# Five bias loads of set-up: begun behind the landing of x of batch 0, in place of first on GpSimd's queue

## The chip, the cores and the metric

The kernel runs on one core of one Trainium2 chip. The metric is the device time of one execution in microseconds (us), median of three. A profiled execution gives a trace; its engines are PE (TensorE matmuls), PEld (TensorE weight loads), DVE (VectorE), ACT (ScalarE), POOL (GpSimd) and SP (SyncE). A letter q behind an engine's name means its queue of instructions, which also issues DMAs. "L199" is line 199 of the kernel before the change.

## What is computed

Two graph layers on x of shape 32 x 512 x 512 in float32, with one adjacency matrix adj of 512 x 512 for all 32 batches:

```python
h = jnp.maximum(_layernorm(x, axis=-1), 0.0)
x = x + _L0_gnn_ref(h, adj, L0_gnn_weight, L0_gnn_bias)
h = jnp.maximum(_layernorm(x, axis=-1), 0.0)
x = x + _L1_gnn_ref(h, adj, Wq, bq, Wk, bk, Wv, bv, Wo, bo)
```

Layer 0 is `(adj @ h) @ weight + bias`. Layer 1 is attention with 8 heads, whose scores get `(1 - adj) * -1e9` added, so that with these weights of adj each row's softmax picks the one key with the largest entry of adj. The attention then is a choice of rows, and its two products with Wv and Wo fold into one with Wv @ Wo. The biases bq and bk enter only through a bound that says whether this short cut holds.

## The kernel before

Set-up (lines 73 to 310) runs once. It loads the weights, adj and x of the first batches into SBUF, multiplies Wv by Wo into `wvo` on TensorE, transposes adj into `adjT`, finds each row's largest entry of adj, checks that the short cut holds (`flag`), and computes batch 0's normalization and its product with adj. Then a value that all engines load from `flag` picks a path, and `single_path` runs over the 32 batches, with a list of work per batch written out step by step. TensorE is fed there by products of 128x128 by 128x256 and the like.

The whole of set-up is under a manual schedule: each engine runs its instructions in the order in which the program writes them, and waits on semaphores for what it reads. So the place of a line in the program is its place in its engine's queue.

The loads of set-up, by queue:

- SyncE: half of Wv's rows 0 to 255 (line 90); Wo's first and third 128 rows and Wv's third (line 93); adj and x of batch 0 in two halves each (line 96, `adj_s` and `xs[0]`); wq, wk, the weight of layer 0 `w0_s`, and x of batch 1 (line 98), 1 MB each.
- ScalarE: the other half of Wv's rows 0 to 255, Wo's second and fourth 128 rows, Wv's fourth (lines 90 and 93).
- GpSimd: after the identity matrix and two constants (lines 99 to 101) the five bias loads of lines 198 to 201: `bv_c`, `bt[0]` (bq) and `bt[1]` (bk) as columns, 512 values each spread over 128 partitions, so that neighbours in a partition lie 128 values apart in memory; `b0_r` and `cvo` (bo) as one row of 2 KB repeated to 128 partitions, 256 KB each in SBUF. They are written far down in the program, but nothing of GpSimd stands before them except the constants, and they wait for nothing.

TensorE's queue starts with twenty transposes of the identity (line 170), then `turn(0, 0)` and `turn(0, 1)`, which transpose Wv's rows 0 to 255 (line 126), one product (`fold`, line 150), `turn(1, 0)` and `turn(1, 1)` with Wv's rows 256 to 511, and the other products of Wv @ Wo with seven block products in place of eight. ScalarE and VectorE copy the transposes to `wvT` (lines 130 and 131), VectorE forms sums of blocks (line 141, and lines 329 to 335 in `sum_a`), and adds products up (lines 184, 205, 214). Then come the largest entries of adj (`peaks`, lines 157 and 158), the statistics of x (lines 361 to 370), the transposes of adj (line 115) and the product with adj (line 271).

Readers of the biases: `bt` is read by ScalarE at line 241, `bv_c` by VectorE at lines 162 and 164, `cvo` at line 293, and `b0_r` at line 300. `w0_s` is first read by sums at lines 341 and 343, x of batch 1 at line 394. Line 673 is the first product of batch 0 in `single_path`, line 312 the load of `flag` on every engine.

Of the kernel before, what the change touches and what calls it, by code (L numbers as in the profile page):

```python
# [8 lines left out]
F32 = mybir.dt.float32  # L9
# [9 lines left out]
P = 128  # L19
# [7 lines left out]
def gnn_two_layers(ctx: ExitStack, tc: tile.TileContext, x, adj, w0, b0, wq, bq, wk, bk, wv, bv, wo, bo, out):  # L27
# [15 lines left out]
    nc = tc.nc  # L43
    B, N, D = x.shape
    C = N // P
# [4 lines left out]
    def big(name):  # L50
        return keep.tile([P, C, N], F32, name=name)

    xs, hs = [big(f"x{i}") for i in range(5)], [big(f"h0_{i}") for i in range(2)]
# [19 lines left out]
    with ExitStack() as tmp, tc.manual_schedule():  # L73
        look = tmp.enter_context(tc.tile_pool(name="look", bufs=1))
# [4 lines left out]
        wt = [look.tile([P, DC, D], F32, name=f"wt{i}") for i in range(2)]  # L79
        bt = [look.tile([P, DC], F32, name=f"bt{i}") for i in range(2)]  # L80
        bv_c = look.tile([P, DC], F32, name="bv_c")
        wvT = yT
        wvT_t = xs[2].rearrange("p c (a n) -> p c a n", a=2)
        wo_t = wvo_t.rearrange("p t c (k n) -> p t c k n", k=2)
# [110 lines left out]
        norms[0].offset()  # L195
        norms[1].stats(1)
        norms[1].power()
        for t, d in ((bv_c, bv), (bt[0], bq), (bt[1], bk)):
            nc.gpsimd.dma_start(t, d.rearrange("(c p) -> p c", p=P))  # L199
        for d, r in ((b0, b0_r), (bo, cvo)):  # L200
# [1462 lines left out]
```

## Time and profile before

| | |
|---|---|
| median of three executions | 1021.16 us (1020.17 to 1023.55) |
| the profiled execution's own time | 1016.16 us |
| its span, first to last instruction | 1014.4 us |
| mean granted TensorE clock | 0.992 |
| GpSimd issues its first bias load at | 1.61 us |
| GpSimd issues its fifth bias load at | 4.62 us |
| bv from issue to landing | 6.4 us |
| b0 from issue to landing | 8.1 us |
| first product of batch 0 (line 673) | 45.27 us |

Times within an execution count from the start of the span. The busy shares of a page are averages over the whole span; set-up is its first 45 us, so what happens in it has to be read from the timeline and from tables of short windows. In a table of windows each engine has its busy time and, in brackets, its instructions; then follow the granted TensorE clock (1.00 is full), the mean busy share of the 16 DMA engines, and GB/s. In a view of the DMA queues, q1 holds SyncE's transfers, q10 ScalarE's, and q0 GpSimd's; the last figure is the time that their packets took, as a share of 16 engines over the window. Packets that overlap on an engine can bring the sum over 100%.

### The profile page before, as it was taken

The numbers are of one execution on the slowest core, as the hardware profiler recorded it, in microseconds if no ns is written. First come the engines' busy times: TensorE is split into PE (matmuls) and PEld (weight loads), VectorE is DVE, ScalarE is ACT, GpSimd is POOL, SyncE is SP. The second block draws the span as 40 slices with busy tenths as digits, with TensorE's granted clock in tenths as the row PEclk, the third lists the DMA queues.
The fourth block names the chain that finished last, engine by engine and source line by source line (L and its number), as shares of the span: only waits on it lengthen the run. The fifth ranks groups of instructions, "written<-read, shape, count | busy, mean of one in ns | idle before, by whom it ended". The sixth has DMA issues, their size and how long they took to land.

```text
span 1014.4 us, 17265 instructions
## 1 busy us (share of the span) xinstructions
PE 988.0 (97%) x5627; PEld 886.9 (87%) x5627; DVE 801.9 (79%) x1792; ACT 586.1 (58%) x1282; POOL 591.1 (58%) x666
## 2 busy tenths in 40 slices
PE   7999999998999999999999999999999999999994
PEld 6468999897999999999999999999999999999882
DVE  4998897667888877778887777788877777888773
ACT  2765364556755555667655555676555556675330
POOL 1032366656666666666666666666766666667543
PEclk8999999999999999999999999999999999999998
DMA  9214558788888888888888888998888888888867
GB/s 312 82 65 152 113 164 250 220 223 219 207 226 206 201 221 209 231 221 207 211 194 207 219 207 227 225 223 202 201 203 213 209 219 227 221 209 207 210 209 265
DMA packets 161884, 208.90 MB, mean 206 GB/s; under 512 B 16556, under 2 KB 104376, under 8 KB 161784
## 3 DMA queue, kind: packets, MB, share of 16 engines
q0 software_dynamic: 44544, 120.10, 48.5%
q1 hardware_dynamic: 115480, 85.66, 29.2%
q10 hardware_dynamic: 1760, 1.93, 0.5%
q8 instruction: 46, 0.75, 0.3%
q14 instruction: 54, 0.44, 0.2%
HBM read 123.55 MB, written 84.09 MB: 205 GB/s over the span
## 4 chain that ended last, share of the span: by engine, by line
PE 72%; DMA 2%; POOL 2%; issue 2%; DVE 1%; ACT 1%; SPq 0%; POOLq 0%; ACTq 0%; DVEq 0%
PE mm L532 50%; PE mm L652 13%; PE mm L655 7%; PE mm L649 2%; DMA hc<-hs 1%; POOL x L495 1%; DMA pi<-posd,idx 1%; DMA z<-zr 1%; DMA hs<-h,dest 0%; POOL hs L692 0%; POOL out_dram L516 0%; POOL yT L495 0%; PE mm L727 0%; ACT h L379 0%; DVE st L361 0%
## 5 line engine op out<-in xcount | busy, mean ns | idle before, releaser
L588 DVE TENSOR_TENSOR x<-mm,x 128x512 f32<-128x512 f32 x217 | 148.8, 686 | 130.2 <-PE mm L532 128.2
L495 POOL DMA_INDIRECT x<-z,pplace x96 | 153.5, 1599 | 81.8 <-ACT yT L660 40.9
L379 ACT ACTIVATE h<-x,off,rstd 128x512 f32<-128x512 f32 x256 | 196.1, 804 | 7.3 <-DVE off L370 4.0
L532 PE MATMUL mm<-w_t,sel 128*128 128x256 f32 x744 | 171.7, 380 | 1.3 <-DVE x L588 1.3
L365 ACT ACTIVATE rstd<-mv,eps 128x2 f32<-128x2 f32 (+1 forms) x90 | 26.3, 292 | 241.8 <-DVE mv L362 241.8
L532 PEld LDWEIGHTS mm<-w_t,sel 128*128 128x128 f32 x744 | 140.6, 190 | 21.4 <-DVE x L588 2.5
L361 DVE BATCH_NORM_STATS2 st<-x 128x6 f32<-128x512 f32 x234 | 157.7, 674 | 1.1
L652 PE MATMUL mm<-ap,h 128*128 128x256 f32 x648 | 157.8, 380 | 0.0
L516 POOL DMA_INDIRECT out_dram<-x,xi x100 | 124.8, 1248 | 42.5 <-DVE zs L578 21.0
L495 POOL DMA_INDIRECT x<-in_x_dram,xi x108 | 104.0, 963 | 72.5 <-DVE x L588 37.4
L652 PEld LDWEIGHTS mm<-ap,h 128*128 128x128 f32 x648 | 114.9, 191 | 11.1
L495 POOL DMA_INDIRECT at<-in_x_dram,gi x81 | 76.9, 949 | 72.8 <-DVE st L361 25.0
L532 PE MATMUL mm<-w_s,yT 128*128 128x256 f32 x496 | 117.3, 379 | 0.8 <-ACT zs L580 0.8
L532 PE MATMUL mm<-hTs,wvo_t 128*128 128x168 f32 x720 | 113.4, 307 | 2.4 <-ACT zs L580 1.4
L532 PEld LDWEIGHTS mm<-hTs,wvo_t 128*128 128x128 f32 x720 | 105.4, 190 | 3.1 <-ACT zs L580 1.9
L580 ACT ACTIVATE zs<-mm,cvo_c 128x168 f32<-128x168 f32 x240 | 83.0, 398 | 38.2 <-PE mm L532 37.8
L532 PEld LDWEIGHTS mm<-w_s,yT 128*128 128x128 f32 x496 | 92.8, 190 | 12.3 <-ACT zs L580 1.0
L655 PEld LDWEIGHTS mm<-ag,adjT 128*128 128x128 f32 x648 | 89.3, 191 | 5.6
L655 PE MATMUL mm<-ag,adjT 128*128 128x128 f32 x648 | 89.7, 275 | 0.0
L627 DVE TENSOR_TENSOR x<-x,b_r 128x512 f32<-128x512 f32 x124 | 84.0, 678 | 0.0
L660 ACT COPY yT<-mm 128x512 f32<-128x512 f32 x108 | 61.5, 571 | 29.6 <-PE mm L655 29.6
L532 PE MATMUL mm<-hT,wvo 128*128 128x168 f32 x480 | 78.3, 306 | 0.0
(323 smaller groups left out, 1678.7 us busy)
## 6 DMA issues: line engine op xcount, KB each, us to landing
hc<-hs SPq DMA_DIRECT2D x124, 176.0 KB
z<-zr SPq DMA_DIRECT2D x120, 96.0 KB
hs<-h SPq DMA_DIRECT2D x52, 192.0 KB
z<-zr SPq DMA_DIRECT2D x120, 80.0 KB
hs<-h SPq DMA_DIRECT2D x52, 160.0 KB
out_dram<-x SPq DMA_DIRECT2D x26, 256.0 KB
x<-in_x_dram SPq DMA_DIRECT2D x12, 256.0 KB
x<-xn SPq DMA_DIRECT2D x8, 256.0 KB
```

Source lines behind the costliest of these rows:

```text
L361: self.nc.vector.bn_stats(st, self.src[:, self.chunks[i], :])
L365: self.nc.scalar.activation(self.rstd[:, 0:len(self.chunks)], self.mv[:, :, 1], AF.Sqrt, bias=self.eps)
L379: self.nc.scalar.activation(dst, src, AF.Relu, bias=self.off[:, i:i + 1], scale=self.rstd[:, i:i + 1])
L495: return behind(nc.gpsimd.indirect_dma_start(out=dst, out_offset=None, in_=rows, in_offset=bass.IndirectOffsetOnAxis(ap=at, axis=0), **more))
L516: stored = behind(nc.gpsimd.indirect_dma_start(out=out_rows, out_offset=bass.IndirectOffsetOnAxis(ap=plan.xi[:, b, c:c + 1], axis=0), in_= ...
L532: nc.tensor.matmul(bank[:, m, 0:half], lhs[:, k, m * P:(m + 1) * P], rhs[:, k, :], start=(first and m == 0 and k == 0), stop=(k == 1), ski ...
L580: taken = nc.scalar.activation(dst[:, m, :], bank[:, m, :], AF.Identity, bias=cvo_c[:, 2 * i + m:2 * i + m + 1])
L588: return nc.vector.tensor_add(dst, bank, dst)
L627: nc.vector.tensor_add(X[b][:, c, :], X[b][:, c, :], b0_r)
L652: nc.tensor.matmul(two(bank, j), H0[b][:, j, cols], two(plan.ap[:, j, :], j), start=False, stop=False, skip_group_check=True)
L655: nc.tensor.matmul(bank[:, j * P:(j + 1) * P], extra[:, j - 1, cols], plan.ag[:, j - 1, j * P:(j + 1) * P], start=False, stop=(j == C - 1) ...
L660: tick(nc.scalar.copy(yT[:, d, :], bank))
```

## The change

A tile `hold` of one column is new. Before its five loads GpSimd copies one column of x of batch 0 into it, from the last 128 rows. These come with the second of x's two halves, so the copy waits for that DMA; the loads stand behind it in GpSimd's queue. Nothing reads `hold`. The order on the other engines and queues is as before. Behind the five loads, GpSimd's next instruction is the load of `flag` (line 312).

```diff
         bv_c = look.tile([P, DC], F32, name="bv_c")
+        hold = look.tile([P, 1], F32, name="hold")
...
         norms[1].power()
+        nc.gpsimd.tensor_copy(hold, xs[0][:, C - 1, 0:1])
         for t, d in ((bv_c, bv), (bt[0], bq), (bt[1], bk)):
             nc.gpsimd.dma_start(t, d.rearrange("(c p) -> p c", p=P))
         for d, r in ((b0, b0_r), (bo, cvo)):
```

## The prediction

> **What bounds the kernel now.** I read the page first, in the order of its parts: the busy shares, then the 40 slices.
>
> ```profile
> PE 988.0 (97%) x5627; PEld 886.9 (87%) x5627; DVE 801.9 (79%) x1792; ACT 586.1 (58%) x1282; POOL 591.1 (58%) x666
> ...
> PE   7999999998999999999999999999999999999994
> ...
> PEclk8999999999999999999999999999999999999998
> ```
>
> TensorE is busy at 9 tenths or more almost throughout; only the first slice (25.4 us) shows both a low share and a low clock. The change sits in that slice. So the question is what set-up waits for, and whether an earlier end of set-up is kept: after it TensorE is the bound, nothing there runs by an absolute clock, and a shift of its first batch matmul should reach the end in full.
>
> Next, the timeline of TensorE alone through set-up (start, duration, engine, line, what it writes and reads, count, and in brackets idle time and releaser):
>
> ```profile
> 5.08 1.04 PE L126 MATMUL pt<-ident,x 128*128 128x128 f32 x8
> 6.14 2.02 PE L150 MATMUL mm<-x,yT 128*128 128x256 f32 x8
> 11.70 0.47 PE L126 MATMUL pt<-ident,x 128*128 128x128 f32 x1 [3.53 <-DMA x<-in_L_gnn_Wv_dram]
> 12.38 1.75 PE L126 MATMUL pt<-ident,x 128*128 128x128 f32 x7 [0.21 <-DMA x<-in_L_gnn_Wv_dram]
> 13.93 3.62 PE L150 MATMUL mm<-x,yT 128*128 128x256 f32 x8
> 17.34 3.96 PE L150 MATMUL mm<-wvo_t,x 128*128 128x256 f32 x16
> ...
> 45.27 4.96 PE L673 MATMUL mm<-w_s,yT 128*128 128x512 f32 x11 [0.72 <-ACT yT L274]
> ```
>
> One long stall, 3.53 us, for rows 256 to 511 of Wv. From 11.70 on there is no other stall of that kind until 45.27, where batch 0 begins. The same shapes also run slower after the stall: 8 products in 3.62 us against 2.02 us before it. A table of the granted clock shows why (columns: busy time and count of PE, PEld, DVE, ACT, POOL, then the clock, DMA share, GB/s):
>
> ```profile
> 8.00:10.00 2.00, 0.17 (x1) 0.00 (x0) 1.07 (x2) 0.59 (x1) 0.00 (x0) 1.00 1.01 318
> 10.00:12.00 2.00, 0.30 (x1) 0.18 (x1) 0.82 (x2) 0.00 (x0) 0.00 (x0) 0.80 0.83 203
> 12.00:14.00 2.00, 1.79 (x9) 1.62 (x9) 0.00 (x0) 0.65 (x2) 0.00 (x0) 0.50 0.98 339
> ...
> 16.00:18.00 2.00, 2.00 (x6) 1.56 (x5) 1.28 (x3) 0.00 (x0) 0.00 (x0) 0.50 1.05 393
> ```
>
> The clock is halved soon after the stall and is full again by about 18.2. Last, what the DMA engines did while TensorE stalled, from 6 to 12 us:
>
> ```profile
> DMA packets 795, 1.51 MB, mean 251 GB/s; under 512 B 178, under 2 KB 178, under 8 KB 795
> ...
> q0 software_dynamic: 230, 0.48, 48.3%
> q1 hardware_dynamic: 300, 0.55, 27.5%
> q10 hardware_dynamic: 265, 0.48, 21.8%
> ```
>
> q0 is GpSimd's queue, so the bias loads: they hold 48.3% of the 16 engines for 6 us and move only 0.48 MB. q1 (SyncE) and q10 (ScalarE), which carry Wv and Wo, get the rest. The same view gives 367 GB/s from 4 to 6.4 us, before q0 sets in, and 376 GB/s from 12 to 28 us, after it.
>
> [...] Here 3.53 us of idleness is followed by 0.50. [...]
>
> **The change, part by part.**
> *Removed from the start.* By 6.4 us, 0.54 (2 to 4 us) and 0.88 MB have moved, 1.42 MB of the 2.10 MB of Wv and Wo (eight transfers of 256 KB, with 2 MB counted as 2.10). Without q0 the other 0.68 MB takes 0.68/0.367 = 1.85 us. q1 lacks 0.30 MB and q10 0.38 MB: at half the rate each, q1 has its last at about 8.0, and q10, sharing with adj at the end, at about 8.5. From last byte to transposes took up to 1 us (q10's last packets lie in the slice 10 to 12, its reader starts at 12.38) on disturbed engines; I take 0.6, so the two readers can start at 8.7 and 9.2 in place of 11.70 and 12.38. TensorE is free at 8.16, so this stands. Gain 3.2 us.
> *Clock.* With 0.5 us idle in place of 3.5 the clock should stay full. 7 transposes then take 7/8 of 1.04 = 0.9 us, not 1.75; 8 products 2.0, not 3.62. TensorE is then done with them at 9.2 + 0.9 + 2.0 = 12.1, and line 150's sixteen start there in place of 17.34: 5.2 us earlier.
> *What is late next.* VectorE. ScalarE's four copies follow the transposes at 0.27 us each and end at about 10.95 (14.82 before), so line 329 starts at 11.0 for 14.85; after three sums of 0.69 it meets line 184, whose 0.72 us wait for products is gone. From there it is 4.5 us ahead, line 362's last ends at 19.0 for 23.48, and line 205 begins at 19.1 for 24.01, without its 0.53 us wait: 4.9 us ahead. TensorE waits for VectorE at lines 265 and 270 (0.26 and 0.76 us before), so the smaller shift rules: **4.9 us**.
> *adj and x.* They follow on q1: 2.10 MB more at 376 GB/s is 5.6 us, so x's second half has landed at 8.25 + 5.6 + 0.6 = 14.4. Line 361 wants it at 17.0 (21.54 less 4.5), adj's first half is wanted at 14.3 and lands near 10.3. No new wait.
> *Added: the copy.* No GpSimd copy is in the trace. A memset of 128x1 took 0.10 us there; I bound the copy by 0.1 and 0.6 (the larger selects of the same engine took 0.58) and take 0.2. It blocks GpSimd from about 1.6 to 14.4; behind it are only the five loads, then the flag at 41.8, so nothing else is held.
> *Moved: the loads.* Their issues took 0.95, 0.80, 0.77, 0.58, 0.58, in sum 3.68 us: 14.6 to 18.3. Landing took 6.4 us for bv and 8.1 for b0. So bv lands at 21.0, bq 21.9, bk 22.7, b0 25.2, bo 25.7. The readers, 4.9 or 5.0 us earlier than before: bq at line 241 25.2, bv at line 162 26.5, bk 27.7, bo at line 293 35.2, b0 at line 300 38.3. The tightest slack is bq's 3.3 us.
> *What they now collide with.* wq, wk, w0 and x of batch 1, 4.2 MB, alone from 13.8 to 25.0. The bias traffic costs what it cost before: 0.53 MB is 1.4 us, and 5.6 us at 244 in place of 376 GB/s (6.4 to 12 us) is 2.0 us; so they end by about 28.4. x of batch 1 is read at line 394, 36.64 less 4.9 = 31.7, and w0 at 31.9. Hidden, with 3.3 us to spare. If that cover failed, each us of lateness beyond it would come off the gain.
>
> Against the profiled execution (1016.16 us, span 1014.4) the sum is 1016.16 - 4.9 = 1011.3. The median is 5.0 us above that execution, and I take the shift from the median: 1021.16 - 4.9 = **1016.3 us**.
>
> **The rivals.**
> *The clock falls all the same.* [...] For it: TensorE was busy only 3.6 of the 6.8 us before the drop. [...] If half clock still covers about 11.4 to 18.2, it then covers dense work: 6.8 us of it loses 3.4, so 5.2 - 3.4 = 1.8 us are left, 1019.4.
> *The weights aren't limited by q0.* Then Wv comes no sooner, the stall stays, and the time is 1021.2 as before. Against it: q1 and q10 together moved 1.03 MB in the 6 us, 172 GB/s, where they had 367 without q0. A half effect, 2.4 us, gives 1018.8.
> *The wait moves to the biases: slower.* Place: ScalarE's line 241 for bq. VectorE is busy while GpSimd issues, among it tensor_scalar and two-input operations, and SyncE has 4.2 MB queued. From 25.2 on each us of lateness costs a us; at 30.1 the gain is used up. bq would need 14.6 us from issue at 15.5, against 6.4 to 8.1 measured. Later in the kernel GpSimd's indirect transfers land in 3.3 to 7.5 us beside a busy VectorE and 80% DMA load, which speaks against it. Landing at 32 gives 1021.16 + 1.9 = 1023.1.
>
> **How the numbers follow.** About 0.3%, 3.1 us, is what a measurement can tell from no change: 1018.1 and 1024.2. The forecast, 4 to 6.5 us of gain, gets 0.68; the clock rival 0.13; little or half effect 0.12; slower 0.07. Faster: the forecast plus 0.09 of the next two, whose better halves reach 3.1 us, 0.77. Slower by over 0.3% needs bq later than 33.2 or something unforeseen: 0.06. Same: 0.17. The range of the likeliest, with a reader start 0.5 us either way and an execution spread of about 1.5 us, is 1014.3 to 1018.3; taking in the clock rival, 1014.0 to 1019.5.
>
> **What would show it.** Right: no DMA wait over 1 us at line 126, q0 absent before 14 us, clock 1.00 from 8 to 20 us, line 673 first at about 40.4, no wait at lines 241, 162, 293, 300. Wrong: line 126 still stalls on Wv; a clock of 0.50 inside dense work; ScalarE idle before line 241 on a DMA; or line 673 earlier by 5 us and the end not.

## The result, and the profile after

The changed kernel takes 1015.69 us (median of 10, 1015.05 to 1019.83) against 1021.56 us before (median of 10): a ratio of 0.9952, with a 95% interval of 0.9937 to 0.9967, so 4.9 us less (3.4 to 6.4). The two medians lie 5.9 us apart and the means of the ten executions 5.0; the ratio and its interval are those on record. Its profiled execution took 1015.4 us, with a span of 1013.7 us.

Line numbers move by one from line 82 and by two from line 198 on: lines 126, 150 and 673 of before are 127, 151 and 675 here. TensorE's timeline through set-up, after:

```profile
5.75 1.75 PE L127 MATMUL pt<-ident,x 128*128 128x128 f32 x8
7.34 1.96 PE L151 MATMUL mm<-x,yT 128*128 128x256 f32 x8
9.13 1.04 PE L127 MATMUL pt<-ident,x 128*128 128x128 f32 x8
10.00 1.89 PE L151 MATMUL mm<-x,yT 128*128 128x256 f32 x8
11.80 3.72 PE L151 MATMUL mm<-wvo_t,x 128*128 128x256 f32 x16
...
39.90 7.11 PE L675 MATMUL mm<-w_s,yT 128*128 128x512 f32 x16 [0.72 <-ACT yT L276]
```

The stall for Wv is gone: the second eight transposes follow the first products without a wait. They take 1.04 us, the products behind them 1.89 us, where before they took about 2.2 and 3.62. The first product of batch 0 comes at 39.90 us, 5.37 us earlier. Only the start is slower than in the trace before: the first eight transposes took 1.75 us where they took 1.04 before, and the first products end at 9.30 in place of 8.16.

Windows of the same trace; the third number from the end is the clock, the last GB/s:

```profile
8.00:10.00 2.00, 2.00 (x14) 1.79 (x14) 1.97 (x4) 0.85 (x3) 0.00 (x0) 1.00 1.05 400
12.00:14.00 2.00, 2.00 (x10) 1.77 (x10) 2.00 (x4) 0.17 (x1) 0.00 (x0) 1.00 1.06 389
```

No half clock behind the weights, and 400 GB/s where there were 318. The DMA view from 6 to 12 us has no q0 any more, and moves 2.39 MB in place of 1.51:

```profile
DMA packets 1269, 2.39 MB, mean 398 GB/s; under 512 B 104, under 2 KB 104, under 8 KB 1269
...
q1 hardware_dynamic: 1006, 1.91, 84.7%
q10 hardware_dynamic: 263, 0.47, 20.5%
```

GpSimd's timeline has the copy and the loads behind it, ScalarE's the first reader of a bias:

```profile
14.27 0.18 POOL L199 COPY hold<-x 128x1 f32<-128x1 f32 x1 [12.71 <-DMA x<-in_x_dram]
14.40 0.95 POOL L201 DMA_DIRECT2D bv_c<-in_L_gnn_bv_dram  x1
...
17.40 0.57 POOL L203 DMA_DIRECT2D cvo<-in_L_gnn_bo_dram  x1
```

```profile
24.50 0.21 ACT L243 ACTIVATE bt<-bt 128x4 f32<-128x4 f32 x1
```

The reader shows no idle time ahead of it. From 12 to 28 us the five loads hold less of the engines than they did at the start:

```profile
DMA packets 2630, 5.24 MB, mean 327 GB/s; under 512 B 212, under 2 KB 212, under 8 KB 2629
...
q0 software_dynamic: 256, 0.53, 11.5%
```

11.5% of 16 us is 1.8 us of every engine. Before, 48.3% of 6 us and 2.1% of the 16 us from 12 on make 3.2 us for the same bytes.

One thing doesn't fit at first sight: the two profiled executions differ by 0.76 us, though the first product of batch 0 gained 5.37 us. The experiments turn to that first.

### The profile page after: what moved, and what is told of

It reads as the page before. It is cut to its first block, busy times and chain, and to the rows that moved or that the text cites. A ratio compares the mean times of both kernels' runs of the same rounds, so it can differ in the third digit from the quotient of the medians.

```text
span 1013.7 us, 17267 instructions
## 1 busy us (share of the span) xinstructions
PE 988.4 (98%) x5627; PEld 886.6 (87%) x5627; DVE 801.1 (79%) x1792; ACT 585.3 (58%) x1282; POOL 590.0 (58%) x667
## 4 chain that ended last, share of the span: by engine, by line
PE 84%; DVE 7%; issue 3%; DMA 3%; ACT 1%; POOL 1%; SPq 0%; POOLq 0%; DVEq 0%; ACTq 0%
PE mm L534 59%; PE mm L654 13%; PE mm L657 7%; PE mm L651 2%; PE mm L675 1%; DVE st L363 1%; DMA hc<-hs 1%; DMA ap<-in_adj_dram,xi 1%; PE mm L273 1%; DVE x L590 1%; DVE x L629 0%; DMA hs<-h,dest 0%; PE pt L171 0%; DMA x<-xn 0%; ACT h L381 0%
```

## The experiments

The theory: the bias traffic delays Wv, TensorE stalls for it, and the stall halves its clock. Ten more runs, e1 to e10, test it. The table puts together what was read from each trace (us from the start of the span), with the ratio to before and its interval. "Wv landed" is when the last of Wv's rows 256 to 511 had landed by the semaphore records of the DMAs, "Wv" when TensorE starts on these rows, which come in two transfers and are begun on with the first, "stall" its wait for them, "half clock" how long the granted clock then was 0.50, "first product" that of batch 0, and "rows" the time from the 320th to the 539th VectorE operation, a stretch of batches between about 137 and 279 us in which rows are first gathered in the new order.

| kernel | Wv landed | Wv | stall | half clock | first product | rows | ratio |
|---|---|---|---|---|---|---|---|
| before | 12.34 | 11.70 | 3.53 | 6.8 | 45.27 | 131.7 | |
| e5 before again | 11.36 | 11.23 | 3.14 | 3.4 | 43.04 | 135.3 | |
| changed | 8.93 | 9.13 | 0 | none | 39.90 | 134.6 | 0.9952 (0.9937 to 0.9967) |
| e1 changed again | 9.27 | 9.11 | 0 | none | 39.78 | 135.8 | 0.9953 (0.9937 to 0.9970) |
| e2 transposes in the stall | 12.22 | 11.75 | filled | none | 42.90 | 135.1 | 0.9983 (0.9970 to 0.9996) |
| e3 columns held | 12.63 | 12.03 | 2.73 | 3.4 | 44.50 | 136.8 | 1.0000 (0.9981 to 1.0018) |
| e4 rows held | 10.80 | 10.64 | 2.17 | 3.4 | 42.66 | 135.6 | 0.9982 (0.9967 to 0.9996) |
| e6 held for Wv | 8.84 | 8.70 | 0 | none | 39.36 | 134.5 | 0.9957 (0.9943 to 0.9970) |
| e7 held for x of batch 1 | 8.80 | 8.65 | 0 | 6.8, from 33.0 | 45.53 | 135.4 | 1.0008 (0.9992 to 1.0024) |
| e8 on SyncE's queue | 8.75 | 8.91 | 0 | none | 39.50 | 138.5 | 0.9962 (0.9948 to 0.9976) |
| e9 rows held, transposes | 11.25 | 11.07 | filled | none | 41.78 | 136.1 | 0.9980 (0.9967 to 0.9994) |
| e10 columns held, transposes | 11.55 | 11.75 | filled | none | 42.28 | 134.5 | 0.9993 (0.9979 to 1.0008) |

Subtract the landing of Wv from the first product, and the twelve traces fall into groups (e7, whose wait comes later, aside). Without half clock, the first product comes 30.5 to 31.0 us after the landing; with 3.4 us of half clock, 31.7 to 31.9; with 6.8 us, 32.9. So what decides set-up is when Wv lands, and on top of it half clock, which costs some 1.2 us in the short spell and 2.2 in the long one.

**e1 and e5: both kernels once more.** No edit.

> The changed kernel once more, for a second trace and beside the others. Theory (bias traffic delays Wv, the delay halves the clock): 0.9952 of before again, line 675 first at 39.5 to 40.5 us, no DMA wait over 1 us at line 127. What is open is where the profiled pair lost 4.7 of the 5.4 us that line 675 gained; if the batches between 140 and 270 us differ from execution to execution, this trace will stand at a third offset there, and if the change costs them something, at the same one.

> The kernel before once more, for a second trace. In five traces the stretch from the 320th to the 540th VectorE operation (batches that first gather rows by the new order) took 131.7 us in the profiled execution before and 134.6 to 136.8 us in the others. If that was a lucky execution, this trace takes 134 to 137 us there, with line 673 at 45 to 46 us as before and a span of 1017 to 1020. Rival (the change costs these batches 3 to 5 us): about 131.7 again.

e5 took 135.3 us in the stretch, e1 135.8. Of twelve traces eleven take 134.5 to 138.5 us, and only the profiled execution before took 131.7. It was a lucky one, in a stretch that the change doesn't touch: there the pair lost 2.9 us of its gain. Another 1.7 us went after the 1699th operation, where the changed execution took longer than its repetition e1 did. What made the one fast and the other slow is not shown. From the 539th operation to the 1699th both kernels take 658.92 us, to the hundredth, so what set-up gains is kept there. The first product in e5 missed the expected 45 to 46 us, and its span of 1016.1 us the expected 1017 to 1020:

```profile
11.23 1.97 PE L126 MATMUL pt<-ident,x 128*128 128x128 f32 x8 [3.14 <-DMA x<-in_L_gnn_Wv_dram]
12.99 2.62 PE L150 MATMUL mm<-x,yT 128*128 128x256 f32 x8
...
43.04 7.11 PE L673 MATMUL mm<-w_s,yT 128*128 128x512 f32 x16 [0.72 <-ACT yT L274]
```

```profile
12.00:14.00 2.00, 2.00 (x9) 1.82 (x8) 0.08 (x1) 1.29 (x4) 0.00 (x0) 0.50 0.96 319
14.00:16.00 2.00, 2.00 (x10) 1.73 (x9) 1.97 (x4) 0.00 (x0) 0.00 (x0) 0.88 1.06 410
```

Here half clock ended before 15, not at about 18 as in the first trace; the eight products took 2.62 us, not 3.62. So what the stall costs before the change differs by some 2 us between executions, of which Wv's landing makes 1.0 us and the clock 1.25. Set side by side, the two pairs of traces give 5.4 us (45.27 less 39.90) and 3.3 us (43.04 less 39.78); the 4.8 or 4.9 us of the ratios lie between.

**e2: the clock alone.** Before, with TensorE kept busy in the stall; the loads stay.

```diff
         nc.scalar.copy(blk(wvo, 0, 0), u)
+        for i in range(24):
+            nc.tensor.transpose(idle[:, i % 4, :], ident, ident)
         turn(1, 0)
```

> Before, with 24 identity transposes on TensorE in the stall and the loads left as they were: the clock alone. Theory: Wv still lands for the transposes at about 11.7 and 12.4 us, but they and the 8 products behind them run at full clock, which takes about 2.4 us off TensorE and, since VectorE's copies gain less, 1.5 to 2.4 us off line 673; ratio 0.9977 to 0.9985. Rival (the gain is all landing): line 673 stays at 45.3, ratio 1.000. Rival (the gain is all clock, the landing is hidden): 5 us, 0.995.

```profile
9.13 2.78 PE L178 MATMUL pt<-ident 128*128 128x128 f32 x24
11.75 0.27 PE L126 MATMUL pt<-ident,x 128*128 128x128 f32 x1
12.26 0.98 PE L126 MATMUL pt<-ident,x 128*128 128x128 f32 x7 [0.24 <-DMA x<-in_L_gnn_Wv_dram]
13.08 1.89 PE L150 MATMUL mm<-x,yT 128*128 128x256 f32 x8
```

Wv's last rows come as late as before, but the transposes and products behind them run at full clock (1.00 from 12 to 16 us; the eight products take 1.89 us, where they took 3.62 before). 0.9983 is 1.7 us (0.4 to 3.1) of the 1018.9 us of before in that comparison; the whole change is 4.8 there. By these figures the clock is about a third of the gain and earlier weights, by difference, about two thirds; the interval leaves the shares wide. Both rivals, no clock at all (1.000) and all clock (0.995), lie outside it. The traces agree if the landing is taken off: the first product of e2 comes only 0.14 us before that of e5, but with Wv landing 0.86 us later.

**e3 and e4: the loads by halves.** In e3 b0 and bo are issued first and the three column loads stand behind the copy; in e4 the columns come first, and b0 and bo stand behind it.

```diff
-        nc.gpsimd.tensor_copy(hold, xs[0][:, C - 1, 0:1])
         for t, d in ((bv_c, bv), (bt[0], bq), (bt[1], bk)):
             nc.gpsimd.dma_start(t, d.rearrange("(c p) -> p c", p=P))
+        nc.gpsimd.tensor_copy(hold, xs[0][:, C - 1, 0:1])
         for d, r in ((b0, b0_r), (bo, cvo)):
```

(the edit of e4, against the changed kernel)

> Only the three column loads (bv, bq, bk) are held; b0 and bo are issued first, at 1.6 us. They have 128 of the 4 KB packets, 2.25 us of every DMA engine's time before, the columns 0.94. Theory (the engines' time counts): the columns' share of the 3.2 us is about 1 us; the stall at line 126 becomes some 2.5 us, and the clock falls or not with it; gain 1 to 3 us, ratio 0.997 to 0.999. Rival (the scattered 4-byte elements are what clogs the engines): nearly the whole gain, 0.995 to 0.996. Rival (the bytes of b0 and bo alone count): 1.000.

> The other half: columns first as before, only b0 and bo held. Theory (engines' time): about 2.25 of 3.2 us of delay go, the stall falls under 1.3 us, the clock stays full; gain 3.5 to 4.8 us, ratio 0.9953 to 0.9966. Rival (the scattered elements clog): little gain, 0.998 to 1.000. Rival (bytes alone): all of it, 0.995.

The stall in e3 was close to the expected 2.5 us; in e4 it was 2.17 where under 1.3 was expected. Both ratios lie outside what was expected, and each is that of a rival: 1.0000 of the one in which b0 and bo alone count, 0.9982 of the one in which the scattered columns clog the engines. Each is refuted by the other run, so both halves count. TensorE in e3 and then in e4:

```profile
12.03 0.33 PE L127 MATMUL pt<-ident,x 128*128 128x128 f32 x1 [2.73 <-DMA x<-in_L_gnn_Wv_dram]
12.67 0.98 PE L127 MATMUL pt<-ident,x 128*128 128x128 f32 x7 [0.32 <-DMA x<-in_L_gnn_Wv_dram]
13.49 3.54 PE L151 MATMUL mm<-x,yT 128*128 128x256 f32 x8
```

```profile
10.64 1.19 PE L127 MATMUL pt<-ident,x 128*128 128x128 f32 x8 [2.17 <-DMA x<-in_L_gnn_Wv_dram]
11.66 3.46 PE L151 MATMUL mm<-x,yT 128*128 128x256 f32 x8
```

b0 and bo alone keep TensorE's start on Wv to 12.03, as late as all five. The columns alone, 6 KB in all, keep it to 10.64, and in e4's DMA view from 6 to 12 us q0 stands with:

```profile
q0 software_dynamic: 96, 0.01, 18.7%
```

18.7% of 6 us, or 1.1 us of every engine, for 0.01 MB. Both stalls, 2.73 and 2.17 us, are followed by a clock of 0.50; the last section shows e4's windows. So neither half alone brings much (0 and 1.8 us), and together they bring 4.8: each half that stays keeps Wv late and, with it, the half clock.

**e9 and e10: the halves with the clock kept.** e4 with 14 and e3 with 24 transposes in the stall, placed as in e2.

> As e4 (only b0 and bo held), with 14 identity transposes in its stall of 2.2 us. Why do the two halves not add up to the whole? Theory: each half alone leaves Wv late enough for the clock to fall, so a half keeps most of the clock's cost. Then with the clock kept, line 675 comes at 41.0 to 41.6, 1.2 to 1.6 us after the changed kernel and 1 us before e4, ratio 0.996 to 0.9975. Rival (half clock is not what the half pays): line 675 at 42.7 as in e4, 0.998.

> As e3 (only bv, bq, bk held), with 24 identity transposes in its stall of 2.7 us. Theory: b0 and bo alone delay Wv to about 12.0 and 12.7 us, as all five do; so with the clock kept line 675 comes at 42.6 to 43.4, as in e2, ratio 0.998 to 0.9995. Rival (the columns add to the delay, and e3's late Wv was chance): Wv by 11.3, line 675 by 42.2, 0.997.

The first product comes at 41.78 and 42.28 us, 0.9 and 2.2 us before e4 and e3. Behind the landing of Wv that is 30.5 and 30.7 us, where e4 and e3 took 31.9: the clock that each half still pays is 1.1 to 1.3 us. The rest is Wv itself, which landed 0.45 us later in e9 than in e4, and 1.1 us earlier in e10 than in e3, though the same loads stood ahead. In e10 the landing of Wv (two transfers, at 11.24 and 11.55) and the first product are nearer to the rival (11.3, 42.2) than to the theory: that Wv came so late in e3 was in part chance. The transposes even outlast the wait there, and hold TensorE until 11.75.

The times don't show the clock. e9 missed both its first product of 41.0 to 41.6 us and its ratio: 0.9980, against e4's 0.9982, is what its rival said, and e10's 0.9993 lies 0.7 us from e3 within overlapping intervals. That each half pays for the clock is thus seen in the traces alone. And the clock is not why the halves don't add up: with it kept in all, e9 and e10 have the first product 1.1 and 0.6 us before e2, the two changed traces 3.0 and 3.1. The delays of Wv themselves don't add: it landed by 9.3 us without these loads, at 10.8 and 11.25 with the columns, at 11.55 and 12.63 with b0 and bo, and at 11.36 to 12.34 with all five. Why is open.

**e6: held for Wv, not for x.**

```diff
-        nc.gpsimd.tensor_copy(hold, xs[0][:, C - 1, 0:1])
+        nc.gpsimd.tensor_copy(hold, wv_s[:, 3, 0:1])
```

> As changed, but the copy waits for Wv's last 128 rows in place of x, so the loads begin at about 9 us in place of 14.4 and share the engines with adj and x of batch 0. Theory (only the delay of Wv counts, and adj and x have 1 to 4 us to spare): line 675 first at 39.8 to 40.8, ratio 0.995 to 0.997. Rival (whatever shares with the loads is delayed by 3 us, and what follows has no room): VectorE waits for x at line 363, line 675 at 41 to 43, 0.997 to 0.999. Of the packets: if they are slow because of the two hardware queues beside them, the column packets take 0.04 to 0.1 us as in the changed kernel, since one of these queues is done; if because they are the kernel's first software transfers, 0.2 to 0.4 us.

```profile
8.89 0.28 POOL L199 COPY hold<-x 128x1 f32<-128x1 f32 x1 [7.33 <-DMA x<-in_L_gnn_Wv_dram]
```

The copy's end of wait is a reading of when Wv's last 128 rows land undisturbed: 8.9 us. The loads begin 5 us earlier than in the changed kernel and share with adj and x of batch 0, and nothing waits for these; the ratio is that of the changed kernel, and the first product (39.36) comes a little before the expected 39.8 to 40.8. So the delay of Wv is what counted, and x was a later bar than needed.

**e7: held for x of batch 1.** The same line with `xs[1][:, C - 1, 0:1]`. It forces the prediction's slow rival.

> As changed, but the copy waits for x of batch 1, the last transfer of set-up: it starts at about 24 to 25 us, bq is issued at about 25.5 and lands near 31, where ScalarE wants it at 24.5. This is the slow rival of the prediction, forced. Theory: ScalarE idles 5 to 7 us before the line that reads bq, TensorE waits for its copies, line 675 at 43 to 46, ratio 0.998 to 1.002, so the point from which holding loses all lies near x of batch 1. Rival (other slack hides it): line 675 under 42, 0.997 or less.

ScalarE's first reader of a bias, and TensorE:

```profile
29.72 0.20 ACT L243 ACTIVATE bt<-bt 128x4 f32<-128x4 f32 x1 [5.55 <-DMA bt<-in_L_gnn_bq_dram]
```

```profile
34.01 0.59 PE L267 MATMUL few<-used,ones 128*128 128x4 f32 x2 [3.25 <-DVE used L282]
34.97 3.76 PE L273 MATMUL mm<-adjT,h 128*128 128x512 f32 x4
...
45.53 4.96 PE L675 MATMUL mm<-w_s,yT 128*128 128x512 f32 x11 [0.72 <-ACT yT L276]
```

The wait moves to bq and, on VectorE, to bv (3.21 us idle there). TensorE's stall of 3.25 us ends with VectorE's line 282, which bv's wait makes late: TensorE comes to line 267 at 34.01 in place of 31.28, and at half clock (0.63 in the mean from 32 to 36 us, 0.52 from 36 to 40) four matmuls of line 273 then take 3.76 us in place of 1.96. Of the 5.6 us that the first product loses against the changed kernel, 2.7 are lost by line 267 and 2.9 behind it. The copy started at 26.05, later than the expected 24 to 25. Ratio 1.0008 (0.9992 to 1.0024): all of the gain is given back.

**e8: on SyncE's queue.** GpSimd loads nothing in set-up; SyncE's queue has the five behind x of batch 0, without copy or wait.

```diff
+        for t, d in ((bv_c, bv), (bt[0], bq), (bt[1], bk)):
+            nc.sync.dma_start(t, d.rearrange("(c p) -> p c", p=P))
+        for d, r in ((b0, b0_r), (bo, cvo)):
+            nc.sync.dma_start(r, bass.AP(tensor=d.tensor, offset=d.offset, ap=[[0, P], [1, D]]))
         for t, w in [(wt[0], wq), (wt[1], wk), (w0_s, w0)] + [(xs[1], x[1])] * (B > 1):
```

> Before, with the five loads taken from GpSimd and written into SyncE's queue behind x of batch 0, with no copy and no wait of their own. Theory (what counts is that they come behind Wv on the DMA engines, not who issues them): line 673 at 39.5 to 40.5 and 0.995 to 0.996, as the changed kernel. Rival (the column loads as single elements hold up the queue they stand in): wq, wk, the weight or x of batch 1 come late, ScalarE or VectorE wait for them, line 673 over 41.

First product at 39.50, ratio 0.9962, within the changed kernel's interval. The loads' place behind the weights counts, and neither the copy nor the engine that issues. No version here beat the changed kernel beyond the intervals; e6 and e8 stand level with it.

## Why the prediction was right

*The stall, and what it is for.* Right. In the changed kernel Wv's last two transfers landed at 8.74 and 8.93 us, where I had their readers at 8.7 and 9.2. TensorE came to them at 9.13 without waiting.

*TensorE free at 8.16.* Wrong in this execution, without harm. I took the first transposes and products to run as in the trace before. They ran 1.1 us later, since TensorE was slow for longer at the start (1.75 us for the first eight transposes, 1.04 before). That 9.13 meets my 9.2 is luck: it is TensorE's own lateness, not the landing.

*The clock stays full.* Right: 1.04 and 1.89 us for transposes and products, where I had 0.9 and 2.0. That half clock is a cost by itself is shown by e2. The slower transposes and products, of which I took off 2.4 us, came from the one trace with the long half-clock spell, and 1.7 us (0.4 to 3.1) is what the times give. I also had half clock begin soon after the stall; it began at 11.20, half a us before the stall's end. What sets that moment is not shown; the last section has what was measured.

*VectorE is late next.* Line 207, formerly 205, began at 18.98 where I had 19.1. TensorE's weights did wait for VectorE at line 267 (1.0 us), as I had it at line 265 of before. The first product came at 39.90, predicted 40.4: a shift of 5.4 us, not 4.9, in this pair.

*The copy and the moved loads.* Start 14.27 (14.4), copy 0.18 us (0.2), issues from 14.40 to 17.97 (14.6 to 18.3). By the semaphore records bv, bq, bk, b0 and bo landed at 20.11, 22.76, 22.95, 24.06 and 25.15 us (21.0, 21.9, 22.7, 25.2, 25.7). No reader waits, as I had it, but bq's reader came 1.7 us after the landing, where I had 3.3. The term that was mis-sized is the cost of the bias traffic in its new place: I carried over what it cost at the start, but it held each engine 1.8 us in place of 3.2. It put off x of batch 1 by 2.7 us (28.65 in the changed kernel, 25.99 in e7, where the biases come behind it), not by 3.4. That x landed about when I said (28.4) is luck: alone it took a us longer than my 25.0. Its reader came at 30.86, so the cover was 2.2 us, not 3.3.

*The slow rival's point.* I put the loss of the whole gain at bq landing at 30.1. In e7 the reader starts at 29.72 and the ratio is 1.0008, within half a us of that point. But the place was wrong, and the agreement is luck: TensorE waited for VectorE, and so for bv, not for what ScalarE does with bq, and about half of the loss came behind that wait, at half clock. I had priced neither. GpSimd's issues in the changed kernel were also no slower beside a VectorE that was busy for 3.86 of the 4 us from 14 to 18 (3.6 us for the five, as before, where VectorE's first operation came behind them, at 6.12), and bv landed 5.7 us after its issue, where it took 6.4 before; so these runs show no slowing of GpSimd beside a busy VectorE, from which this rival started.

*The sum.* 4.9 us off the median was predicted, and 0.9952 is 4.9 us of 1021.56. To the tenth that is luck: 4.9 was read from the trace with the long half-clock spell, and set-up itself gained 5.4 us in that pair and 3.3 in the other. The other sum, 1011.3 for the profiled execution, failed (1015.4): it took that execution's later batches for typical, and their gathering stretch was some 3 us faster than in any other trace.

## What to carry to other kernels

Where the first matmuls of a kernel wait for weights, as here, try small loads behind the weights on the DMA engines, whichever engine issues them (0.9952 from GpSimd, 0.9962 from SyncE here); count the share of the engines that they hold, not their bytes (18.7% of 6 us for 0.01 MB in e4). Ask then by when each is read: the room between the last weight and the first reader was wide here (loads begun at 9 us in e6 or at 14 in the changed kernel made no difference, 26 in e7 lost all). And holding a part of them may bring little, as in e3 (0 us) and e4 (1.8 of 4.8), if what stays is enough to keep the weights late and half clock with them.

## What the runs showed of the hardware

TensorE's stalls for Wv of 2.17, 2.73, 3.14 and 3.53 us (e4, e3, e5, before) were each followed by a clock of 0.50, and so was the stall of 3.25 us in e7. Where transposes filled the stall (e2, e9, e10), and where there was none (the changed kernel, e1, e6, e8), the clock column says 1.00 up to 20 us.

Half clock neither begins nor ends with the stall. In before it began at 11.20, half a us ahead of the stall's end, and lasted to 18.03; TensorE was busy for 6.12 of these 6.83 us. In e4 the stall was over at 10.64, and half clock began 1.2 us later, in dense work. Windows of e4; the first number behind the comma is TensorE's busy time, the third from the end the clock:

```profile
8.00:10.00 2.00, 0.47 (x3) 0.07 (x1) 0.83 (x2) 0.59 (x1) 0.00 (x0) 1.00 0.97 327
10.00:12.00 2.00, 1.36 (x10) 1.23 (x11) 1.06 (x2) 0.57 (x3) 0.00 (x0) 0.96 1.05 391
12.00:14.00 2.00, 2.00 (x6) 1.62 (x5) 1.31 (x3) 0.62 (x3) 0.00 (x0) 0.50 1.05 388
14.00:16.00 2.00, 2.00 (x8) 1.64 (x7) 1.52 (x4) 0.00 (x0) 0.00 (x0) 0.69 1.05 387
```

It lasted 3.4 us in e3, e4 and e5, and 6.8 us in e7 and before, whose stalls were the longest two (3.25 and 3.53 us). In the first 3.4 us of half clock TensorE still idled 0.71 us in before and about 1.0 us in e7, but only about 0.2 us in e5. Whether the stall or this idle time made it last longer was not tested, and what sets its begin is not shown.

The same 6 KB of columns cost quite different times. In the DMA records their packets of 128 bytes have a median of 0.21 us before, 0.41 in e4 and 0.23 in e7, but 0.04 in the changed kernel, e3 and e6. Neither of the two causes that I put forward in e6's expectation holds: in e7 they are slow with no other load beside them, and in e6 and the changed kernel they are fast though they are the first of their kind. The cause stays open.

How long TensorE is slow at the start differs from execution to execution: the first eight transposes of Wv took 1.04 us in both traces of before, and 1.75 and 1.47 us in the two of the changed kernel, while the clock column says 1.00 in all four. It isn't the change that does it: e4, e6 and e7 have 1.04 us, and e2, which has the loads of before, 1.68. In before the first clock record, one of full clock, stands at 4.38 us, ahead of these transposes (5.08); in the changed kernel's trace it stands at 7.21, behind their start (5.75). So for these transposes the column's 1.00 is a recorded clock in the one and not in the other.
